# First queries and keys of the second layer loaded beside the scan's end, and a new order for that layer

## The chip, the core and the metric

The kernel runs on one core of a Trainium2 chip. The core has five engines with instruction streams of their own: TensorE (PE; its weight loads are listed as PEld), VectorE (DVE), ScalarE (ACT), GpSimd (POOL) and SyncE (SP), which here issues nearly all DMAs. Each engine runs its stream in order and waits on semaphores; the DMAs of a queue are moved by 16 DMA engines. The metric is the time of one execution in microseconds on the device, lower being better.

## What is computed

Two layers stand one behind the other, each added to its input. x has 4 batches of 1024 tokens with 512 features.

The first layer is a selective scan over time with 16 states and 1024 inner channels:

```python
def step(h, inputs):
    ad, bd, xt, ct = inputs
    h = jnp.clip(h * ad[:, :, None] + bd[:, :, None] * xt[:, None, :], -10.0, 10.0)
    yt = jnp.einsum('bd,bdh->bh', ct, h)
    return (h, yt)
...
x = x + (ys + D * xn) * silu(gate) @ W_out.T
```

In outline, the second layer is attention with 16 heads of 32 features, with weights that are scaled per batch by a style:

```python
q = heads(einsum('bsh,oh->bso', x, q_weight) * q_dc[:, None, :])
k = heads(einsum('bsh,oh->bso', x, k_weight) * k_dc[:, None, :])
v_flat = einsum('bsh,oh->bso', x, v_weight) * v_dc[:, None, :] * s2[:, None, :]
attn = softmax(einsum('bhqd,bhkd->bhqk', q, k) * scale)
out = einsum('bhqk,bhkd->bhqd', attn, heads(v_flat))
return out @ w (scaled by w_dc) + v_flat @ u (scaled by u_dc)
```

In the second layer x is first scaled by the style and normalized over its features.

## The kernel before

**The scan.** `mamba` goes through the 1024 time steps in chunks of 64. For each step SP spreads a row of 256 KB over the partitions (`rep<-xnd`, function `spread`, six buffers), ScalarE scales it (`u`), VectorE makes the step (`g`), and TensorE sums four steps into `yb`. Behind the scan come, for each half chunk, transposes (`yt`), a product with the gate on VectorE or GpSimd (`xnT`), and the output projection (`po`), whose sum with x goes to DRAM (`x1d`).

**The head of the second layer.** Beside the last chunks runs `overlapped` (L1050), which prepares what of the second layer is possible already: the norm of the first blocks of batch 0 (`hio`, `hntr`, result `xs`), the scale factors (`hraw`, `dc`), and queries and keys of two groups of four heads for the first 512 tokens. Each such result is split into two parts, a high one (`hfh`) and the rest (`hfl`), and written to a bounce buffer in DRAM (`bnc`). Its instructions take place among those of the scan by the scheduler's choice. Buffers of 128 x 4096 numbers named w00, w01, w10 and w11 are shared by both layers: in the scan they hold the input weights, afterwards `xs` (w00, w01), the values (w10) and the output weights `wo` (w11).

**The second layer.** `attention` works in units: 4 batches of 8 units, each one group of four heads by 512 queries. For each unit there are

- loads of queries `qs` (three buffers), keys `ks` and key differences `ds` (two buffers each, for the two units of a group) from the bounce buffer; a load takes three DMAs, one for each third of 96 partitions (`stack`, L1350). A 97th row holds the negative row maximum for the queries (`qs<-mt`) and ones for the keys (`ks<-oned`);
- the row maxima: `dps` and `mps` on TensorE, `r` on ScalarE and VectorE (`peaks`), for the very first unit a plain maximum `mx` (`first_peaks`, L1297);
- scores `st`, exponents `p`, sums `s` on GpSimd (VectorE takes one head of four), products with the values `avs`, the ratio `ao`.

Between these lies other work, which the text calls fillers: norm (`io`, `st`, `mv`, `ntr`), queries and keys (`heads`: `wqr`, `wqh`, `wql`, `qps`, `fh`, `fl`), values (`raw`, `bc`, `wh`, `wl`, `vps`), the skip product (`skip`: `vt`, `ups`, with weights `wo`) and the output product.

**What sets the order.** The order of the second layer is written by a planner, `Loom` (L44): generators name an engine, a duration and conditions, and the planner picks the one that can start first, ties by rank. The instructions of each engine are then chained in that order (`Lane`), so that on the chip each engine runs the planned sequence whatever the real durations are. The ranks of the fillers come from `DUE` and `DUE0` (batch 0), counted in exponents, 32 to a unit; `EXTRA` is a latency that the planner adds for work off the main chain.

At the start of the layer the planner isn't asked. The rows of ones and the loads of the first queries and keys are issued by SP ahead of everything else, at a high priority:

```python
with tc.high_priority(offset=FIRST):
    for t in ks:
        nc.sync.dma_start(out=f32(t[96:97].rearrange("o h t -> o (h t)")), in_=E.oned)
    ...
    for nm, dst in (("q", qs[0]), ("k", ks[0][:, :, 0:512])):
        for y in stack(0, 0, nm, 0, dst):
            pass
```

The buffers `qs` and `ks` belong to pools of the second layer, which lie where pools of the scan were.

Of the kernel before, what the change touches and what calls it, by code (L numbers as in the profile page):

```python
# [39 lines left out]
def f32(ap):  # L40
    return ap.bitcast(F32)
# [811 lines left out]
EARLY = -10  # L853
CORE = ("scores", "exponent", "groups", "alone", "sums", "ratio", "peaks", "peak", "row", "first_peaks", "first_peak")
LAT1 = {'PE': 0.3, 'ACT': 0.4, 'DVE': 0.8, 'POOL': 0.8, 'SP': 4.0, 'L1': 0.0}
EXTRA = {'PE': 0.1, 'ACT': 0.3, 'DVE': 0.3, 'POOL': 0.5, 'SP': 1.0}
MARGIN = 0.9
END = (12, 3, 12)
LAND = {"q": 5.5, "k": 9.0, "d": 10.5}
DUE = {'norm': (-206, 14.4), 'heads': (-96, 24), 'v0': (-108, 2.2), 'v1': (12, 2.2), 'skip': (100, 8), 'out': (266, 9)}  # L860
DUE0 = {'heads': (-72, 24), 'v0': (-10, 2.2), 'v1': (40, 2.2)}
FIRST = 1000000

class Env:
# [23 lines left out]

    def values(self):
        self.v = self.sp.tile([128, 8, DM], F32, tag="w10", name="v")
        self.wv = self.sp.tile([128, 2, 2, 4, 256], F32R, tag="w11", name="wv")

    def out_weights(self):
        self.wo = self.sp.tile([128, 2, 2, 4, 256], F32R, tag="w11", name="wo")
# [153 lines left out]
def overlapped(E, *L0):  # L1050

    wk, pm, E.pe, E.vec, E.act = L0
    E.light = True
    raws, turns = [0], [1]

    def tile(name, shape, dt=F32):
        n = int(np.prod(shape[1:]))
        if name in ("g", "qps") and (name == "g" or turns[0] % 3 == 0):
            turns[0] += name == "qps"
            t = pm[0].tile([128, 512], F32, tag=pm[2], name="hg")  # L1060
        elif name == "ntr" or name == "qps" and turns[0] % 3:
            turns[0] += 1
            t = pm[0].tile([128, 512], F32, tag=pm[1], name="h" + name)
        else:
            if name == "raw":
                raws[0] ^= 1
            tag, full, dd, bufs = {
                "raw": ("xh", [128, 4, 256], F32R, 2) if raws[0] else ("xl", [128, 4, 256], F32R, 2),
                "small": ("cv", [128, 4, 64], F32, 3), "bc": ("cv", [128, 4, 64], F32, 3),
                "s1": ("xc", [128, 2, 2, 4, 32], F32, 4), "io": ("xr", [128, 2, 4, 67], F32, 5),  # L1070
                "st1": ("st", [128, 4, 6], F32, 2), "mv1": ("mv", [128, 4], F32, 2),
                "wqr": ("xr", [128, 2, 4, 67], F32, 5), "tmp": ("xc", [128, 2, 2, 4, 32], F32, 4),
                "wqh": ("xc", [128, 2, 2, 4, 32], F32R, 4), "wql": ("xc", [128, 2, 2, 4, 32], F32R, 4),
                "fh": ("tok", [128, 1024], F32R, 2), "fl": ("tok", [128, 1024], F32R, 2)}[name]
            t = wk.tile(full, dd, tag=tag, name="h" + name, bufs=bufs)
            d = " ".join("abcd"[:len(full) - 1])
            t = t if dd == dt else f32(t)
            t = t.rearrange("p %s -> p (%s)" % (d, d)) if len(full) > 2 else t
        t = t[:shape[0], 0:n]
        return t.rearrange("p (a b) -> p a b", a=shape[1]) if len(shape) == 3 else t  # L1080

    E.tile = tile
    E.inputs()
    yield from norm_x(E, 0, range(4))
    yield from demodulation(E)
    yield from heads(E, 0, (0,), (0, 1))
    yield from norm_x(E, 0, range(4, 7))


def attention(ctx, E, T, out, begun):  # L1090
# [34 lines left out]
    def mark(*key):  # L1125
        done[key] = loom.end

    def have(*key):
        return lambda: done.get(key)
# [12 lines left out]
    def parts():  # L1142

        j = frs.take()
        return j, tuple(work(x, [128, 512], 1, F32R, f"{x}{j}") for x in ("fh", "fl"))

    def place(u, qq=0, kp=0, h=0):
        return 32 * u + 16 * qq + 4 * kp + h

# [2 lines left out]
    def scores():  # L1152
        for u in range(NU):
            for qq, kp, h in np.ndindex(2, 4, 4):
                yield "PE", 0.25, sts, have("row", u), have("k", u // 2, 0), have("k", u // 2, 1)
                i = sts.take()
                q, k = qs[u % 3], ks[u // 2 % 2]
                st = pst.tile([128, 2, 256], F32, tag="t", name="st")
                for e in range(2):
                    kb = 2 * kp + e  # L1160
                    pe.matmul(st[:, e, :], k[0:97, h, kb * 128:kb * 128 + 128], q[0:97, h, qq * 256:qq * 256 + 256], start=True, stop=True)
                loom.add(exponent(u, qq, kp, h, i, st), place(u, qq, kp, h))
            mark("scores", u)

# [119 lines left out]
    def row(u, m1):  # L1284
        yield "PE", 0.15, bank_of
        i, tr = bank([16, 128], "mtr")
        pe.transpose(tr, m1.rearrange("p h q -> p (h q)"), ident)
        yield "ACT", 0.2, mts
        j, mt = mts.take(), work("mt", [16, 128], 1, F32R)
        acte.activation(mt, tr, AF.Identity, scale=-1.0)  # L1290
        bank_of.give(i)
        yield "SP", 0.6
        sp.dma_start(out=f32(qs[u % 3][96:97].rearrange("o h (q c) -> o (h q) c", c=128)), in_=f32(mt))
        mts.give(j)
        mark("row", u)

    def first_peaks():  # L1297

        q, k = qs[0], ks[0]
        mx = work("mx", [128, 4, 4, 2], 1)  # L1300
        for o, h, qb in np.ndindex(2, 4, 4):
            yield "PE", 0.24, bank_of, have("q", 0), have("k", 0, o)
            i, ps = bank([128, 512], "mps")
            pe.matmul(ps, q[0:96, h, qb * 128:qb * 128 + 128], k[0:96, h, o * 512:o * 512 + 512], start=True, stop=True)
# [12 lines left out]
    def peaks():  # L1317

        for u in range(1, NU):
            m1 = work("m1", [128, 4, 4], 2)  # L1320
            left[u] = 16
            for h, qb in np.ndindex(4, 4):
                n = (u - 1) * 16 + h * 4 + qb
                yield "PE", 0.24, bank_of, past("relu", n - RF), have("q", u), have("k", u // 2, 0), have("d", u // 2)
                i, ps = bank([128, 512], "dps")
                qh = qs[u % 3][0:96, h, qb * 128:qb * 128 + 128]
                pe.matmul(ps, qh, ds[u // 2 % 2][:, h, :], start=True, stop=True)
                loom.add(peak(u, n, i, ps, qh, h, m1[:, h, qb:qb + 1], m1), 2 * n + EARLY)

    def peak(u, n, i, ps, qh, h, m, m1):  # L1330
# [4 lines left out]
        mark("relu", n)  # L1335
        yield "PE", 0.24, bank_of
        i, ps = bank([128, 512], "mps")
        pe.matmul(ps, qh, ks[u // 2 % 2][0:96, h, 0:512], start=True, stop=True)
# [21 lines left out]
    def loads():  # L1360
        for u in range(NU):
# [205 lines left out]
            mark(key, b)  # L1567

    def skip_weight(b):
        yield "SP", 0.01, have("values", b, 1), past("out", b - 1)  # L1570
        for hf in range(2):
            yield from weight("u", b, hf)
        mark("wu", b)
# [5 lines left out]
        mark("wo", b)  # L1579

    def skip(b, tb):
        w = [(E.wo[:, hf, 0], E.wo[:, hf, 1]) for hf in range(2)]
# [12 lines left out]
        i, ps = yield from project(vh, vl, w)  # L1595
        ts.give(k)
        yield "DVE", 0.62
        dve.tensor_tensor(out=x1, in0=ps, in1=x1, op=ALU.add)
# [28 lines left out]
        return rs, ao, j, jo  # L1627

    def output(b, tb, n):
        w = [(E.wo[:, hf, 0], E.wo[:, hf, 1]) for hf in range(2)]  # L1630
# [10 lines left out]
        i, ps = yield from project(ah, al, w)  # L1641
        ts.give(k)
        yield "DVE", 0.62
        dve.tensor_tensor(out=rs, in0=ps, in1=rs, op=ALU.add)
# [6 lines left out]

    def ending(b, tb):

        w = [E.wo[:, :, e] for e in range(2)]

        def products(ps, ah, al, kb):
            for n, (a, e) in enumerate(((ah, 0), (ah, 1), (al, 0))):
                pe.matmul(ps.rearrange("p (h c) -> p h c", h=2), a, w[e][:, :, kb, :], start=kb == 0 and n == 0, stop=kb == 3 and n == 2)
# [37 lines left out]


    loom.end = 0.0
    with tc.high_priority(offset=FIRST):
        for t in ks:  # L1700
            nc.sync.dma_start(out=f32(t[96:97].rearrange("o h t -> o (h t)")), in_=E.oned)
# [12 lines left out]
    loom.add(first_peaks(), -100)  # L1714
    loom.add(style(0), -91)
    for tb in range(begun, NT):
# [69 lines left out]
```

## Time and profile before

| | us |
|---|---|
| median of 3 executions | 2790.56 |
| lowest and highest | 2787.77 and 2792.78 |
| the profiled execution | 2796.49 |
| its span, first to last instruction | 2794.7 |
| PE busy | 2566.8 (92%) |
| ACT busy | 2021.2 (72%) |
| DVE busy | 1994.9 (71%) |
| POOL busy | 2083.1 (75%) |
| last step of the scan ends | 1275.2 |
| first scores of the second layer | 1365.2 |

The profile is of one execution. Busy time is the time in which an engine runs at least one instruction; issuing a DMA isn't counted. "Granted clock" is the share of full speed that TensorE's clock had, here 0.951 in the mean. The chain of waits follows the work that ended last back from the end: at each piece to what released it. In the timeline a group is given with its start, its length, its engine and its tiles (out<-in), and in brackets the idle time of the engine before it with what ended it. Nearly all instructions have the line of a helper, L167, so tiles are what tells them apart.

### The profile page before, as it was taken

What the parts mean: (1) busy time and instruction counts of PE and PEld (TensorE: products, weight loads), DVE (VectorE), ACT (ScalarE), POOL (GpSimd) and SP (SyncE); (2) the same over time, 40 slices, a digit from 0 to 9 for tenths busy, and PEclk for the clock granted to TensorE, in tenths of its full rate; (3) what the DMA queues carried; (4) which work ended last, traced back from release to release, by engine and by line L of the source; (5) the groups of instructions that cost most, each with busy time, mean ns of one, the idle gap of its engine ahead of it and who ended that gap; (6) DMA issues with size and microseconds to landing.
All of it is one profiled execution on the core that took longest, in us unless ns stands there. A gap on an engine that the chain in (4) does not pass through costs nothing.

```text
span 2794.7 us, 54619 instructions
## 1 busy us (share of the span) xinstructions
PE 2566.8 (92%) x18421; PEld 1775.8 (64%) x18421; DVE 1994.9 (71%) x3518; ACT 2021.2 (72%) x3766; POOL 2083.1 (75%) x2365
## 2 busy tenths in 40 slices
PE   7798999999999998886989899989999899999998
PEld 7565565665566665433756677756777667777765
DVE  4778888888878887674557766677567786667665
ACT  5888888888888888663567677667766676676674
POOL 5887788787778787443378888787787787777786
PEclk9899999999999999787989999999999999999998
DMA  5789989999989999895652455344553545345422
GB/s 173 226 239 273 271 267 274 274 265 272 270 250 272 273 276 266 254 252 147 174 130 82 121 141 171 104 127 116 147 144 118 135 124 140 120 121 151 107 58 91
DMA packets 333772, 518.26 MB, mean 185 GB/s; under 512 B 33514, under 2 KB 108586, under 8 KB 333362
## 3 DMA queue, kind: packets, MB, share of 16 engines
q1 hardware_dynamic: 333076, 514.71, 65.1%
q8 instruction: 145, 2.38, 0.4%
q14 instruction: 135, 1.11, 0.1%
q10 hardware_dynamic: 416, 0.07, 0.0%
HBM read 422.35 MB, written 92.05 MB: 184 GB/s over the span
## 4 chain that ended last, share of the span: by engine, by line
PE 43%; DMA 15%; POOL 15%; ACT 11%; DVE 8%; issue 7%; SPq 0%; ACTq 0%; POOLq 0%; DVEq 0%
DMA rep<-xnd 9%; PE avs L167 8%; PE st L167 7%; POOL s L167 5%; ACT u L167 5%; PE ups L167 5%; PE qps L167 4%; DVE g L167 4%; PE mps L167 3%; PE ps L167 3%; POOL tmp L167 3%; PE vps L167 3%; PE dps L167 3%; POOL tm L167 2%; PE po L167 2%
## 5 line engine op out<-in xcount | busy, mean ns | idle before, releaser
L167 DVE CUSTOM_DVE_ANT_0 g<-g,u,hi 128x512 f32<-128x512 f32 x1024 | 820.5, 801 | 209.4 <-ACT u L167 171.3
L167 ACT ACTIVATE p<-st 128x512 f32<-128x512 f32 x1024 | 599.2, 606 | 312.3 <-PE st L167 288.6
L167 ACT ACTIVATE u<-rep,bd 128x512 f32<-128x512 f32 x1024 | 699.4, 689 | 121.5 <-DMA rep<-xnd 67.8
L167 POOL TENSOR_TENSOR s<-s,p 128x512 f32<-128x512 f32 x384 | 538.9, 1420 | 58.1 <-ACT p L167 57.2
L167 DVE CUSTOM_DVE_ANT_0 r<-mps,r 128x512 f32<-128x512 f32 x496 | 334.7, 683 | 271.9 <-PE mps L167 249.7
L167 PE MATMUL ps<-xh,w_in 128*128 128x256 f32 x2048 | 493.4, 317 | 15.2 <-ACT w_in L167 10.5
L167 PE MATMUL st<-qs,ks 97*128 97x256 f32 x2048 | 450.5, 305 | 33.1 <-ACT p L167 24.0
L167 PEld LDWEIGHTS st<-qs,ks 97*128 97x128 f32 x2048 | 350.1, 195 | 152.4 <-ACT p L167 82.8
L167 POOL TENSOR_TENSOR s<-p 128x512 f32<-128x512 f32 x192 | 255.1, 1342 | 202.2 <-PE avs L167 106.9
L167 PEld LDWEIGHTS ps<-xh,w_in 128*128 128x128 f32 x2048 | 344.8, 191 | 91.7 <-issue 65.3
L167 PE MATMUL yb<-g,sy 128*32 128x512 f32 x2048 | 287.9, 633 | 57.7 <-DVE g L167 42.5
L167 ACT ACTIVATE r<-dps 128x512 f32<-128x512 f32 x496 | 298.5, 606 | 42.2 <-DVE m L167 20.5
L167 POOL TENSOR_TENSOR tmp<-tmp,tm 128x256 f32<-128x256 f32 x372 | 272.6, 733 | 73.6 <-ACT tmp L167 44.6
L167 PE MATMUL ps<-xl,w_in 128*128 128x256 f32 x1024 | 290.2, 283 | 0.0
L167 PE MATMUL avs<-p,v 128*32 128x256 f32 x4096 | 269.8, 408 | 2.4 <-ACT p L167 2.3
L167 PE MATMUL mps<-ks,qs 96*128 96x512 f32 x528 | 222.3, 435 | 16.1 <-DMA ks<-bnc 9.7
L167 PEld LDWEIGHTS ps<-xl,w_in 128*128 128x128 f32 x1024 | 196.4, 192 | 30.1 <-issue 30.1
L167 PE MATMUL dps<-ds,qs 96*128 96x512 f32 x496 | 204.4, 413 | 11.6 <-DMA bnc<-fh 5.7
L167 PEld LDWEIGHTS avs<-p,v 128*32 128x32 f32 x4096 | 126.8, 116 | 112.6 <-issue 25.4
L167 POOL TENSOR_SCALAR tm<-xr,c_w_conv 128x256 f32<-128x256 f32 x372 | 182.3, 490 | 20.1
L167 PE MATMUL qps<-xs,wqh 128*128 128x512 f32 x480 | 190.1, 401 | 0.1
L167 PE MATMUL ups<-wo,th 128*128 128x256 f32 x960 | 187.8, 288 | 0.0
(389 smaller groups left out, 4826.2 us busy)
## 6 DMA issues: line engine op xcount, KB each, us to landing
rep<-xnd SPq DMA_DIRECT2D x1024, 256.0 KB, 4.8
qs<-bnc SPq DMA_DIRECT2D x96, 256.0 KB, 4.5
ks<-bnc SPq DMA_DIRECT2D x96, 256.0 KB, 7.6
bnc<-fh SPq DMA_DIRECT2D x76, 256.0 KB, 3.3
bnc<-fl SPq DMA_DIRECT2D x76, 256.0 KB, 3.0
xnd<-z SPq DMA_DIRECT2D x64, 256.0 KB, 4.6
io<-x1d SPq DMA_DIRECT2D x57, 256.0 KB, 3.4
ds<-bnc SPq DMA_DIRECT2D x48, 256.0 KB, 9.0
```

The lines of the kernel that those rows point to most:

```text
L167: i = f(*a, **k)
```

## The change

The change has four parts.

1. A new function `first` takes a buffer in the place w11 while the scan still runs. It writes the row of ones of the keys, and after the queries and keys of the first group are in the bounce buffer, loads both into it, three DMAs each. `overlapped` calls it between the first and the second group. The loads at the start of `attention` go, with their high priority.
2. `scores`, `peaks`, `row` and `first_peaks` read the first unit's queries (`E.q0`) and the first group's first 512 keys (`E.k0`) from there. The keys' rows of ones are written when the keys of a group are first loaded.
3. The output weights `wo` take w11 only when the first group's scores are done: `skip_weight` waits for the scores of unit 1.
4. Due places and a latency of the planner have new values. (The second number of an entry of `DUE0` isn't read: the step comes from `DUE`.)

```diff
-EXTRA = {'PE': 0.1, 'ACT': 0.3, 'DVE': 0.3, 'POOL': 0.5, 'SP': 1.0}
+EXTRA = {'PE': 0.1, 'ACT': 0.3, 'DVE': 0.3, 'POOL': 0.25, 'SP': 1.0}
...
-DUE = {'norm': (-206, 14.4), 'heads': (-96, 24), 'v0': (-108, 2.2), 'v1': (12, 2.2), 'skip': (100, 8), 'out': (266, 9)}
-DUE0 = {'heads': (-72, 24), 'v0': (-10, 2.2), 'v1': (40, 2.2)}
-FIRST = 1000000
+DUE = {'norm': (-206, 14.4), 'heads': (-136, 24), 'v0': (-68, 2.2), 'v1': (12, 2.2), 'skip': (100, 8), 'out': (266, 9)}
+DUE0 = {'heads': (-84, 19.2), 'v0': (30, 2.2), 'v1': (40, 2.2)}
...
-        self.wv = self.sp.tile([128, 2, 2, 4, 256], F32R, tag="w11", name="wv")
+    def first(self):
+        t = self.sp.tile([128, 2, 4, 512], F32R, tag="w11", name="first")
+        self.q0, self.k0 = t[0:97, 0], t[0:97, 1]
+        self.nc.sync.dma_start(out=f32(t[96:97, 1].rearrange("o h t -> o (h t)")), in_=self.oned[:, 0:2048])
+        for nm, dst, order in (("q", self.q0, (0, 0, 1)), ("k", self.k0, (0, 1, 0))):
+            for p, e in enumerate(order):
+                self.nc.sync.dma_start(out=f32(dst[32 * p:32 * p + 32]), in_=self.parts[0, 0, nm, 0][e].rearrange("(h p) c -> p h c", h=4))
+                yield
...
-    yield from heads(E, 0, (0,), (0, 1))
+    yield from heads(E, 0, (0,), (0,))
+    yield from E.first()
+    yield from heads(E, 0, (0,), (1,))
...
+    def queries(u):
+        return qs[u % 3] if u else E.q0
+    def first_half(g):
+        return ks[g % 2][:, :, 0:512] if g else E.k0
...
+                if g < 2:
+                    yield "SP", 0.6
+                    sp.dma_start(out=f32(ks[g][96:97].rearrange("o h t -> o (h t)")), in_=E.oned)
...
-        yield "SP", 0.01, have("values", b, 1), past("out", b - 1)
+        yield "SP", 0.01, have("values", b, 1), past("out", b - 1), have("scores", 1)
+        if b == 0:
+            E.out_weights()
...
-    with tc.high_priority(offset=FIRST):
-        for t in ks:
-            nc.sync.dma_start(out=f32(t[96:97].rearrange("o h t -> o (h t)")), in_=E.oned)
-        for hg in range(2):
-            keys[hg] = E.parts[0, hg, "k", 0]
-            for nm in "qk":
-                mark("part", 0, hg, nm, 0)
-        for nm, dst in (("q", qs[0]), ("k", ks[0][:, :, 0:512])):
-            for y in stack(0, 0, nm, 0, dst):
-                pass
-    done["q", 0] = done["k", 0, 0] = 4.0
+    for hg in range(2):
+        keys[hg] = E.parts[0, hg, "k", 0]
+        for nm in "qk":
+            mark("part", 0, hg, nm, 0)
+    E.parts.pop((0, 0, "q", 0)), E.parts.pop((0, 0, "k", 0))
+    done["q", 0] = done["k", 0, 0] = 0.0
...
-    E.out_weights()
```

More of the change, by code (lines that the diff above doesn't have):

```diff
@@ L1156, in scores @@
                 i = sts.take()
-                q, k = qs[u % 3], ks[u // 2 % 2]
+                q, k = queries(u), ks[u // 2 % 2]
                 st = pst.tile([128, 2, 256], F32, tag="t", name="st")
@@ L1160, in scores @@
                     kb = 2 * kp + e
-                    pe.matmul(st[:, e, :], k[0:97, h, kb * 128:kb * 128 + 128], q[0:97, h, qq * 256:qq * 256 + 256], start=True, stop=True)
+                    pe.matmul(st[:, e, :], (first_half(u // 2) if kb < 4 else k[:, :, 512:])[0:97, h, kb % 4 * 128:kb % 4 * 128 + 128], q[0:97, h, qq * 256:qq * 256 + 256], start=True, stop=True)
                 loom.add(exponent(u, qq, kp, h, i, st), place(u, qq, kp, h))
@@ L1292, in row @@
         yield "SP", 0.6
-        sp.dma_start(out=f32(qs[u % 3][96:97].rearrange("o h (q c) -> o (h q) c", c=128)), in_=f32(mt))
+        sp.dma_start(out=f32(queries(u)[96:97].rearrange("o h (q c) -> o (h q) c", c=128)), in_=f32(mt))
         mts.give(j)
@@ L1297, in first_peaks @@
     def first_peaks():
-        q, k = qs[0], ks[0]
+        q = queries(0)
         mx = work("mx", [128, 4, 4, 2], 1)
@@ L1303, in first_peaks @@
             i, ps = bank([128, 512], "mps")
-            pe.matmul(ps, q[0:96, h, qb * 128:qb * 128 + 128], k[0:96, h, o * 512:o * 512 + 512], start=True, stop=True)
+            pe.matmul(ps, q[0:96, h, qb * 128:qb * 128 + 128], first_half(0)[0:96, h] if o == 0 else ks[0][0:96, h, 512:], start=True, stop=True)
             loom.add(first_peak(i, ps, mx[:, h, qb, o:o + 1], o * 16 + h * 4 + qb), -100)
@@ L1325, in peaks @@
                 i, ps = bank([128, 512], "dps")
-                qh = qs[u % 3][0:96, h, qb * 128:qb * 128 + 128]
+                qh = queries(u)[0:96, h, qb * 128:qb * 128 + 128]
                 pe.matmul(ps, qh, ds[u // 2 % 2][:, h, :], start=True, stop=True)
@@ L1337, in peak @@
         i, ps = bank([128, 512], "mps")
-        pe.matmul(ps, qh, ks[u // 2 % 2][0:96, h, 0:512], start=True, stop=True)
+        pe.matmul(ps, qh, first_half(u // 2)[0:96, h], start=True, stop=True)
         yield "DVE", 0.75
@@ L1581, in skip @@
     def skip(b, tb):
-        w = [(E.wo[:, hf, 0], E.wo[:, hf, 1]) for hf in range(2)]
         yield "PE", 0.48, bank_of, ts, ios, have("wu", b)
@@ L1594, in skip @@
         bank_of.give(i)
-        i, ps = yield from project(vh, vl, w)
+        i, ps = yield from project(vh, vl, [(E.wo[:, hf, 0], E.wo[:, hf, 1]) for hf in range(2)])
         ts.give(k)
@@ L1629, in output @@
     def output(b, tb, n):
-        w = [(E.wo[:, hf, 0], E.wo[:, hf, 1]) for hf in range(2)]
         rs, ao, j, jo = yield from places(b, tb, *[have("ao", b, hg, tb // 2) for hg in range(4)])
@@ L1640, in output @@
             aols.give(jo)
-        i, ps = yield from project(ah, al, w)
+        i, ps = yield from project(ah, al, [(E.wo[:, hf, 0], E.wo[:, hf, 1]) for hf in range(2)])
         ts.give(k)
@@ L1652, in ending @@
     def ending(b, tb):
-        w = [E.wo[:, :, e] for e in range(2)]
         def products(ps, ah, al, kb):
             for n, (a, e) in enumerate(((ah, 0), (ah, 1), (al, 0))):
-                pe.matmul(ps.rearrange("p (h c) -> p h c", h=2), a, w[e][:, :, kb, :], start=kb == 0 and n == 0, stop=kb == 3 and n == 2)
+                pe.matmul(ps.rearrange("p (h c) -> p h c", h=2), a, E.wo[:, :, e, kb, :], start=kb == 0 and n == 0, stop=kb == 3 and n == 2)
         rs, ao, j, jo = yield from places(b, tb, *[have("ao", b, hg, tb // 2) for hg in range(3)])
```

## The prediction

> **What bounds the kernel now.** I read the page's engine table first, then busy time by stretch, then the chain of waits, then the timeline of the handover. On the page TensorE is busy 92% of the span and no other engine over 75%, so an idle TensorE is what a gain has to come from. Its idle time lies in two places: at the handover from the scan to the second layer, and in small pieces all through the layer.
>
> The stretches (us, busy time of each engine, granted clock, DMA share, GB/s):
>
> ```profile
> 1250.00:1270.00 20.00, 18.86 (x78) 8.62 (x78) 13.21 (x17) 15.33 (x26) 8.63 (x7) 1.00 1.04 301
> 1270.00:1280.00 10.00, 5.06 (x32) 2.29 (x30) 6.93 (x14) 4.38 (x7) 4.29 (x5) 1.00 0.41 155
> 1280.00:1295.00 15.00, 11.33 (x28) 5.34 (x28) 5.17 (x20) 4.66 (x7) 3.57 (x5) 0.77 0.12 36
> 1295.00:1305.00 10.00, 0.29 (x4) 0.09 (x2) 0.00 (x0) 1.39 (x3) 2.73 (x3) 0.65 0.88 205
> 1305.00:1317.00 12.00, 9.32 (x17) 4.81 (x17) 11.25 (x18) 2.28 (x3) 4.96 (x4) 0.50 0.35 103
> ```
>
> See the fourth row: for 10 us TensorE works 0.29 and VectorE not at all, while DMA runs at 0.88. Just before that, from 1270 to 1295, the DMA engines were nearly free; and before that, in the scan's last 20 us, they were full (1.04).
>
> SP's issues in the timeline of the same place (start, length, engine, what):
>
> ```profile
> 1293.33 2.21 SPq L1701 DMA_DIRECT2D ks<-oned  x2
> 1295.59 1.27 SPq L167 DMA_DIRECT2D qs<-bnc  x3
> 1296.90 1.38 SPq L167 DMA_DIRECT2D ks<-bnc  x3
> ...
> 1299.44 0.63 SPq L167 DMA_DIRECT2D raw<-in_vT  x1
> 1300.12 0.61 SPq L167 DMA_DIRECT2D bc<-dcd  x1
> ```
>
> And the engines' side of it (in brackets the idle time before the group and what ended it):
>
> ```profile
> 1282.32 9.82 PE L167 MATMUL po<-c_wout,xnT__15706 128*128 128x512 f32 x16 [4.27 <-DVE xnT__15706 L167]
> ...
> 1304.95 8.92 PE L167 MATMUL mps<-ks,qs 96*128 96x512 f32 x16 [9.71 <-DMA ks<-bnc]
> 1305.75 9.65 DVE L167 TENSOR_REDUCE mx<-mps 128x1 f32<-128x512 f32 x16 [12.78 <-PE mps L167]
> ...
> 1308.27 1.27 POOL L167 TENSOR_TENSOR raw<-raw,bc 128x512 f32<-128x512 f32 x1 [10.42 <-DMA bc<-dcd]
> ...
> 1315.33 0.68 DVE L167 BATCH_NORM_STATS2 st<-io 128x6 f32<-128x512 f32 x1
> ...
> 1317.19 0.29 PEld L167 LDWEIGHTS vps<-wl,xs 128*128 128x128 f32 x1 [3.17 <-DVE wl L167]
> ```
>
> Eight DMAs are issued by SP ahead of everything else the layer needs; the first products (mps) wait for the last of them. VectorE then reduces 16 products, and only behind these come the norm of the last block (st) and the split of the value weights (wl), which holds TensorE until 1317.19.
>
> The chain of waits through the layer (start, length, what):
>
> ```profile
> 1261.90 6.97 DMA rep<-xnd
> ...
> 1453.08 7.87 DMA qs<-mt
> ```
>
> Both are transfers that the chain waits for: a spread at the scan's end, and in the layer the 8 KB row of maxima, issued behind nine 256 KB loads. The built order leaves these nine there.
>
> **Part 1: six loads leave the gap and go into the scan.** In the built order the six loads of the first queries and keys stand among the last ten spreads (rep). SP meets them in place of idle time, but the DMA engines are full there: six times 256 KB are 1.57 MB, and at the 301 GB/s of the first row that is 5.2 us. Below, the cost is zero if the spreads had slack to spare; above, 5.2 plus a block of SP: the last query load waits for the landing of the bounce hfl (median 5.3 us), and the last spread is issued behind it, at most some 1.8 us late (5.3 less the two spreads and two loads issued in between). ScalarE waits only 3.9 us for spreads between 1250 and 1275, six times, and twice by 0.2 or less, so part of the delay finds slack: I take +3.5, range 0 to 7. [...] The row has a DMA share of 1.04, and I go by the row.
>
> **Part 2: four products before the last output projection.** The built order puts four mps ahead of po, in the 4.27 us in which TensorE waits for VectorE. At about 0.55 us each (8.92 over 16) they take 2.2 us and are hidden, as long as the loads have landed; the last is issued near 1268 and may land 7.6 us later, before 1278. The po then has a gap of about 2.1 us before it. Here po takes 9.82 for 16, 0.61 each, and the clock in its stretch is 0.77. A shorter gap, 2.52 us ahead of the scan's last product at 1275.27, left the clock at 1.00 in the second row; at the later po's pace of 0.43 the 16 take 6.9. So: 0 to -2.9, and I take -2.9 because 2.1 is nearer to the gap that did no harm. [...]
>
> **Part 3: the gap itself.** Without the six loads and one of the two ks<-oned (2.21 for two), SP reaches raw and bc 3.8 us sooner: 1.1 + 1.27 + 1.38. Raw then leaves at 1295.7, bc at 1296.3. With the landing time of this run, 8.15 us from the issue of bc to its use, GpSimd starts at 1304.5 and gains 3.8 at least. With bc's median 4.7 it starts at 1301. VectorE has its 16 reductions from 1293, and is through at 1302.6 (9.65 later) instead of 1315.4. From 1301 GpSimd does raw, wql, raw, io (four times 1.27) to 1306.1, so st starts at 1306.1 for 1315.33: -9.2. ScalarE's wh follows at 1304.8 (1.04 in the timeline), and wl after st at 1306.8, so the vps that waited until 1317.19 starts near 1308: also -9.2. With the slow landing GpSimd ends at 1309.6, st gains 5.8. Range -5.8 to -10.1 (all of wl's 1.2 saved too); I take -9.2 because the crowd of six loads that made the landing slow is gone. What is late next is the landing of raw and bc. The second ks<-oned now stands ahead of the second group's keys, and so of the first row of maxima: 1.1 us of SP, at no cost, because SP sits idle from 1355.45 to the issue of that row at 1358.03; without this cover the first scores, 1365.2, would be 1.1 later.
>
> **Part 4: the order.** New due places and a smaller latency for GpSimd let the planner set the whole layer anew. Count the products between the first scores of one unit and of the next in both built orders, and price each by this chain's rows: scores 0.48 for four, avs 1.86 for 32, qps 0.70 for three, vps and ups 0.71 for six, mps and dps 0.46 for two. A unit's length is the time between the first exponents of one unit and the next in the trace. The work per unit, before and after: unit 2 31.5 and 24.1; unit 5 31.9 and 37.7; unit 17 38.5 and 42.3; unit 20 29.1 and 23.9; unit 21 38.1 and 45.9; unit 26 37.9 and 26.6. The total is the same, the new order less even: above 38 us it has 28 us, the old one 5. Light units don't get shorter than about 40 us (27.5 us of work in unit 29 took 36.2, 29.1 in unit 20 took 40.2, 31.5 in unit 2 took 40.3), heavy ones take 1.16 of their work (44.8 for 38.5). If nothing is smoothed the order costs (28 - 5) x 1.16 = 26. On the other side, the first batch's skip weights now wait for the second unit's scores and move from units 0 and 1 to 1 and 2, which takes two raw at 1.28 from GpSimd in unit 0; and the stall of 7.87 could go. That bounds a gain at 2.6 + 7.9 = 10.5. From -10.5 to +26 I take 0: units overlap through twelve score buffers, light and heavy neighbours (20 and 21, 4 and 5) even out, and lengths between 27.5 and 40 us of work fit one line almost as well as a floor does.
>
> **Sum.** +3.5 - 2.9 - 9.2 + 0 = -8.6. The profiled execution took 2796.49 around a span of 2794.7; the median shown is 2790.56, and I take the difference from that: 2782.
>
> **Rivals.** *The gap is only moved.* The spreads are delayed in full, SP blocks, the po stays slow, raw lands as late as now: +7 - 0 - 5.8 = +1.2, 2791.8. For it: DMA share 1.04 in the very place. Against it: from 1270 on DMA falls to 0.41 and 0.12, so the delayed part ends at once. That the loads don't move at all is excluded by the built order.
>
> *The uneven order decides (slower).* Place: unit pairs such as 20 and 21, with 45.9 us of TensorE work in one. Price 26, less the 8.6 of the handover: +17.4, 2808. It decides from the point where more than 14.2 of the 26 isn't smoothed (8.6 plus 5.6). For it: units 11 and 19, where all the norm transposes fall together, take 53.4 and 53.8. Against: such lumps exist before as well, and 24 to 29 run at 36 to 47.
>
> **Chances and range.** A change under 0.2%, 5.6 us, can't be told from none in this kernel. Forecast 0.50 (2782; alone, 2766 to 2785), the moved gap 0.17, the uneven order 0.33. Faster 0.50, same 0.17, slower 0.33. The range takes in most of the slower case: 2766 to 2808. The best corner, 0 - 2.9 - 10.1 - 10.5 = -23.5, and the worst, +7 - 5.8 + 26 = +27, are left out as both need every term at its end.
>
> **What would show it.** Right: the idle before the first mps falls from 9.71 to below 3; the vps behind wl starts some 8 us nearer to the last step of the scan; po near 7 us; the last u later by 3 to 4. Wrong: the last u later by over 5; raw waiting for bc as long as now; unit 21 over 52 us and unit 20 still 40, or the layer from first scores to end longer than today's 1429 (2794.7 - 1365.2).

## The result and the profile after

The changed kernel takes 2824.78 us (median of 4, 2820.25 to 2836.27), the kernel before on the same chip 2791.67 (2787.77 to 2796.30): a ratio of 1.0120, 95% interval 1.0098 to 1.0142. It is slower by 33 us where 9 us faster was forecast. The profiled execution took 2825.94 around a span of 2824.1, against 2794.7 before.

The same stretches as before, of the changed kernel (us, busy time of TensorE, its weight loads, VectorE, ScalarE, GpSimd, granted clock, DMA share, GB/s):

```profile
1250.00:1270.00 20.00, 16.36 (x65) 6.69 (x64) 9.84 (x13) 10.25 (x17) 2.53 (x2) 0.96 1.06 282
1270.00:1280.00 10.00, 6.90 (x29) 3.10 (x29) 5.42 (x8) 5.97 (x10) 3.52 (x3) 0.83 0.78 219
1280.00:1295.00 15.00, 11.41 (x33) 5.51 (x32) 7.55 (x26) 3.49 (x5) 5.65 (x7) 0.89 0.14 48
1295.00:1305.00 10.00, 6.24 (x20) 2.97 (x20) 9.41 (x16) 3.66 (x7) 5.98 (x5) 0.88 0.57 172
1305.00:1317.00 12.00, 7.91 (x46) 7.41 (x47) 3.98 (x6) 4.08 (x7) 6.13 (x7) 0.67 0.33 100
```

The hole has gone: in the fourth row TensorE works 6.24 us where it worked 0.29, VectorE 9.41 where it worked nothing. The price stands in the first two rows: ScalarE, which works off the spreads, is down from 15.33 to 10.25 in the scan's last 20 us, with the DMA engines as full as before (1.06 for 1.04), and the second row is still busy with transfers (0.78 for 0.41).

The timeline of the same place, changed kernel:

```profile
1281.47 1.17 PE L167 MATMUL mps<-first 96*128 96x512 f32 x4
...
1285.15 8.80 PE L167 MATMUL po<-c_wout,xnT__15706 128*128 128x512 f32 x16 [2.50 <-DVE xnT__15706 L167]
...
1296.81 5.95 PE L167 MATMUL mps<-first 96*128 96x512 f32 x12
...
1307.80 0.69 DVE L167 BATCH_NORM_STATS2 st<-io 128x6 f32<-128x512 f32 x1 [3.21 <-POOL io L167]
...
1309.67 0.29 PEld L167 LDWEIGHTS vps<-wl,xs 128*128 128x128 f32 x1 [1.72 <-DVE wl L167]
```

The products that waited for wl start at 1309.67 where they started at 1317.19, although the scan's last step ended 3.7 us later (1278.88 for 1275.21). The first exponent comes at 1361.04, 4.7 us earlier than before.

So the handover gains and the kernel loses: from the first exponent to the end the layer takes 1463.1 us, before 1428.9, 34 more. The loss isn't spread evenly. Unit 14 alone is 18.2 us longer (63.0 for 44.8). What happens in it (busy time by stretch, then timeline, changed kernel):

```profile
2045.00:2050.00 5.00, 5.00 (x32) 4.00 (x31) 3.90 (x8) 3.92 (x8) 5.00 (x5) 1.00 0.08 28
2050.00:2055.00 5.00, 3.02 (x17) 2.43 (x16) 5.00 (x1) 2.85 (x6) 5.00 (x5) 1.00 0.14 52
2055.00:2060.00 5.00, 0.00 (x0) 0.00 (x0) 5.00 (x1) 0.00 (x0) 5.00 (x6) 0.70 0.77 210
2060.00:2065.00 5.00, 3.69 (x12) 2.87 (x12) 4.55 (x9) 1.20 (x2) 0.10 (x1) 0.50 0.01 3
```

```profile
2049.40 1.28 POOL L167 TENSOR_TENSOR s<-p 128x512 f32<-128x512 f32 x1
...
2049.69 10.96 DVE L167 TENSOR_TENSOR s<-p 128x512 f32<-128x512 f32 x1
2050.65 1.28 POOL L167 TENSOR_TENSOR fh<-fh,fl 128x512 f32<-128x512 f32 x1
2051.90 2.50 POOL L167 TENSOR_TENSOR s<-s,p 128x512 f32<-128x512 f32 x2
...
2058.70 1.40 POOL L167 TENSOR_TENSOR s<-s 128x256 f32<-128x256 f32 x2
2060.57 0.68 DVE L167 CUSTOM_DVE_ANT_0 r<-mps,r 128x512 f32<-128x512 f32 x1
...
2061.31 0.79 PE L167 MATMUL dps<-ds,qs 96*128 96x512 f32 x1 [8.29 <-DVE m L167]
```

One addition on VectorE, of a form whose shortest takes 0.63 us, takes 10.96. It begins while GpSimd is in the middle of a row of instructions without a pause (5.00 of 5.00 us, three stretches running), and it ends 0.55 us after that row does. Everything behind it waits: r on VectorE, dps on TensorE (8.29 us idle), and the granted clock is 0.50 when TensorE comes back. Both operands of this addition lie in SBUF. The reductions r, which read one operand from PSUM, never take over 0.69 us, 496 of them before and 496 after.

Take together VectorE's instructions over 2.5 us in the layer: before 5 of them, 27 us; after 11, 61 us. Of TensorE's idle times over 1 us, those that overlap such an instruction in time sum to 16 us before and 44 after. This was the first theory: **the new order puts GpSimd's work back to back around VectorE's additions**. Its rivals were the uneven units that the prediction had named, and the new handover itself.

### The profile page after: what moved, and what is told of

It is laid out like the page before. It is cut to its first block, busy times and chain, and to the rows that moved or that the text cites. A ratio compares the mean times of both kernels' runs of the same rounds, so it can differ in the third digit from the quotient of the medians.

```text
span 2824.1 us, 54587 instructions
## 1 busy us (share of the span) xinstructions
PE 2576.7 (91%) x18421; PEld 1778.8 (63%) x18421; DVE 2022.7 (72%) x3518; ACT 2019.1 (71%) x3766; POOL 2070.9 (73%) x2365
## 4 chain that ended last, share of the span: by engine, by line
PE 45%; DMA 16%; ACT 12%; POOL 11%; DVE 9%; issue 7%; SPq 1%; ACTq 0%; POOLq 0%; DVEq 0%
DMA rep<-xnd 10%; PE avs L167 8%; PE st L167 8%; PE ups L167 6%; ACT u L167 5%; DVE g L167 5%; PE qps L167 4%; POOL s L167 4%; PE mps L167 3%; PE dps L167 3%; POOL tmp L167 3%; PE ps L167 3%; PE vps L167 3%; ACT p L167 2%; POOL tm L167 2%
## 5 line engine op out<-in xcount | busy, mean ns | idle before, releaser
L167 PE MATMUL st<-qs,ks 97*128 97x256 f32 x1952 | 432.5, 307 | 34.3 <-ACT p L167 27.9
L167 PEld LDWEIGHTS st<-qs,ks 97*128 97x128 f32 x1952 | 334.6, 196 | 154.3 <-ACT p L167 91.2
L167 ACT ACTIVATE r<-dps 128x512 f32<-128x512 f32 x496 | 300.8, 610 | 66.4 <-PE dps L167 38.1
L167 PE MATMUL mps<-ks,qs 96*128 96x512 f32 x480 | 202.7, 427 | 6.2 <-DVE m L167 4.8
```

Of the source, the lines that this page charges most:

```text
L167: i = f(*a, **k)
```

## The experiments

Each ratio is to the kernel before, run between the others on the same chip. "Layer" is the time from the first exponent to the end in the one profiled execution, and "long" the sum of VectorE's instructions over 2.5 us there.

### Which part loses

*structure*: the new handover and the old due places, except one shift without which the planner finds no order.

```diff
-EXTRA = {'PE': 0.1, 'ACT': 0.3, 'DVE': 0.3, 'POOL': 0.25, 'SP': 1.0}
+EXTRA = {'PE': 0.1, 'ACT': 0.3, 'DVE': 0.3, 'POOL': 0.5, 'SP': 1.0}
...
-DUE = {'norm': (-206, 14.4), 'heads': (-136, 24), 'v0': (-68, 2.2), 'v1': (12, 2.2), 'skip': (100, 8), 'out': (266, 9)}
-DUE0 = {'heads': (-84, 19.2), 'v0': (30, 2.2), 'v1': (40, 2.2)}
+DUE = {'norm': (-206, 14.4), 'heads': (-96, 24), 'v0': (-108, 2.2), 'v1': (12, 2.2), 'skip': (100, 8), 'out': (266, 9)}
+DUE0 = {'heads': (-74, 24), 'v0': (-10, 2.2), 'v1': (40, 2.2)}
```

> The changed kernel with the old EXTRA, DUE and DUE0 (but heads of DUE0 at -74 in place of -72): the new handover under an order made by the old places. Theory (GpSimd's back-to-back work holds up VectorE's adds in the new order): the layer is as long as before, 1425 to 1435 us from first exponent to end, the handover gains 4 to 9, so 2782 to 2790; VectorE instructions over 2.5 us sum to at most 40 us. Rival (the structure costs: skip weights that wait for the second unit, loads in the scan): 2810 or more. Rival (uneven order): 2782 to 2790 as well.

1.0067 (1.0042 to 1.0092), layer 1459.5, long 47.4. *order_alone*: the kernel before with the three new lines and nothing else.

> The kernel before with the new EXTRA, DUE and DUE0 and nothing else changed. Theory: the loss is the order's, so 2815 to 2835, and VectorE instructions over 2.5 us sum to 50 us or more, against 27 in the kernel before. Rival (structure): 2785 to 2800. If the order differs from that of the changed kernel and the time is near 2791, the sum of long VectorE instructions should be near 27 again; if the time is high and that sum is low, the theory falls.

1.0154 (1.0111 to 1.0197), 2839.82 us (a little over its bounds), layer 1469.8, long 63.6. *old_latency*: the changed kernel with only EXTRA put back.

> The changed kernel with EXTRA of GpSimd back at 0.5, the new due places kept. Theory: time follows the long VectorE instructions of whatever order comes out; if the smaller latency packs GpSimd's work and is the cause, 2782 to 2795 with a sum under 40; if the due places are, 2815 or more with a sum over 50. Rival (uneven order from the new due places): 2815 or more with a low sum.

1.0184 (1.0147 to 1.0221), layer 1490.8, long 50.5. So the order alone loses what the whole change loses, and putting the old latency back doesn't bring the time back. But structure, whose due places are the old ones but for one, loses as well, and its order isn't the old one: the planner is so sensitive that a shift of two exponents redraws the layer. Hence *before_redrawn*, the kernel before with that shift alone:

```diff
-DUE0 = {'heads': (-72, 24), 'v0': (-10, 2.2), 'v1': (40, 2.2)}
+DUE0 = {'heads': (-74, 24), 'v0': (-10, 2.2), 'v1': (40, 2.2)}
```

> The kernel before with one number changed: heads of DUE0 -74 in place of -72, a shift by two exponents of 1024, which makes the planner set the rest of the layer anew. Theory (any new order loses the luck of the old one, whose long VectorE instructions sum to only 27 us): 2805 to 2830, ratio 1.005 to 1.014, with a sum of 40 us or more. Rival (the new due places are bad in themselves, a neighbouring order of the old places isn't): within 0.3% of before, 2785 to 2800.

1.0136 (1.0103 to 1.0170), layer 1467.1. So a redraw, a new order that comes of a change without a meaning, costs as much as the change does. Yet its long instructions sum to 32.9 us only, under the 40 that the theory asked for: the stalls on VectorE can't be all.

The last doubt on this question is removed by *same_order*. It has the new handover, but planner, places and latencies of before; the second unit reads its keys from their old buffer, loaded behind raw and bc, so that the output weights may take their place after the first unit. ScalarE, VectorE and GpSimd then run the old sequence through the layer, instruction for instruction in the trace.

```diff
+    def first_half(u):
+        return ks[u // 2 % 2][:, :, 0:512] if u else E.k0
...
+        if (b, nm, hf) == (0, "v", 0):
+            for t in ks:
+                sp.dma_start(out=f32(t[96:97].rearrange("o h t -> o (h t)")), in_=E.oned)
+            bnc = E.parts.pop((0, 0, "k", 0))
+            for p, e in enumerate((0, 1, 0)):
+                sp.dma_start(out=f32(ks[0][32 * p:32 * p + 32, :, 0:512]), in_=bnc[e].rearrange("(h p) c -> p h c", h=4))
```

> The new handover under the very order of the kernel before: planner, due places and latencies are those of before, so ScalarE and GpSimd run the same sequence through the whole layer. The first unit reads queries and keys loaded beside the scan's end; the second unit reads the keys from their old buffer, whose three loads (and the rows of ones) SP issues behind raw and bc; the output weights take the place when the first unit is done. Theory (the order loses, not the handover): first exponent 8 to 10 us nearer to the last step of the scan, that step later by 3.5 to 7, the layer 1425 to 1432 long, so 2 to 7 us faster than before, ratio 0.9975 to 0.9995. Rival (the new handover itself unsettles the layer): slower than before, 1.002 or more.

0.9989 (0.9968 to 1.0010), layer 1425.2, and the same five long instructions at the same places as before (27.1 us). The handover costs nothing in the layer; the redrawn order is the loss.

### What a redrawn order loses by

*pool_waits*: the changed kernel in its own order, with GpSimd's next instruction made to wait for VectorE's addition.

```diff
+                if self.eng is self.tc.nc.gpsimd and Lane.port is not None:
+                    self.tc.add_manual_dep(i.ins, Lane.port, AFTER, reason="the port first")
+                    Lane.port = None
...
-            add.tensor_tensor(out=s, in0=P[u, qq, 0, h][1] if first else s, in1=P[u, qq, kp, h][1], op=ALU.add)
+            i = add.tensor_tensor(out=s, in0=P[u, qq, 0, h][1] if first else s, in1=P[u, qq, kp, h][1], op=ALU.add)
+            if h in VADD:
+                Lane.port = i.ins.name
```

> The changed kernel in its own order, but GpSimd's next instruction waits for VectorE's add of three of the four adds of a head's sum (192 waits in all). Theory: no such add takes over 2.5 us any more, their mean falls from 1.26 us to near 1.0; the stall of unit 14 (63 us) goes back to some 45, and the kernel gains 10 to 25 against the changed one, 2800 to 2815, less what GpSimd loses by waiting. Rival (uneven order): adds get shorter but the time doesn't fall, 2820 to 2840.

1.0064 (1.0038 to 1.0090): 15 us gained. VectorE's additions by tile, count, and shortest, median and longest time in ns; the kernel before, the changed kernel, then pool_waits:

```profile
L167 DVE TENSOR_TENSOR s<-s,p x128: 674/938/5103, 1381.9 to 2777.0; 128x512 f32<-128x512 f32 x128
L167 DVE TENSOR_TENSOR s<-p x64: 627/988/1803, 1374.0 to 2766.7; 128x512 f32<-128x512 f32 x64
```

```profile
L167 DVE TENSOR_TENSOR s<-s,p x128: 669/1136/6925, 1375.5 to 2805.8; 128x512 f32<-128x512 f32 x128
L167 DVE TENSOR_TENSOR s<-p x64: 627/978/10958, 1368.7 to 2795.5; 128x512 f32<-128x512 f32 x64
```

```profile
L169 DVE TENSOR_TENSOR s<-s,p x128: 676/1085/1869, 1366.4 to 2783.7; 128x512 f32<-128x512 f32 x128
L169 DVE TENSOR_TENSOR s<-p x64: 628/873/1792, 1359.7 to 2773.3; 128x512 f32<-128x512 f32 x64
...
  POOL s L169: 64.4, 61
```

The longest falls from 10.96 to 1.87 us with the order unchanged, and unit 14 from 63.0 to 48.0. GpSimd's additions wait 64.4 us for it in 61 places (last line: who waited for these instructions, us and times), and still the kernel gains. That VectorE is held up by GpSimd's unbroken work, and that this costs time, is thereby shown. *before_pool_waits*, *after_all_waits* and *structure_all_waits* let GpSimd wait also for the fourth addition and for VectorE's mv, wl, wo and tl, each marked in the same way:

> The kernel before in its own order, with GpSimd's next instruction made to wait for VectorE's instructions of two SBUF operands (adds of sums, mv, wl, wo, tl). A control: the order before has 17 us of TensorE idle time beside long VectorE instructions (after has 44). Theory: a gain of 0 to 15 us, 2775 to 2793, VectorE instructions over 2.5 us nearly gone. Rival (the waits themselves are what gains, or cost): the gain is as large as for the changed kernel, or the kernel loses over 10 us.

0.9977 (0.9961 to 0.9993), layer 1422.0, long 3.1.

> As pool_waits (the changed kernel in its own order), and GpSimd also waits for the fourth add and for VectorE's mv, wl, wo and tl. Theory: the 14.6 us of long VectorE instructions left there go as well, TensorE's idle beside them falls by some 7, and the time falls to 2798 to 2810. Rival: those waits hold GpSimd up as long as they help VectorE, 2811 to 2825.

1.0071 (1.0041 to 1.0102), layer 1441.4, long 9.5: no better than pool_waits in time.

> The run structure (new handover, order of the old places) with the same waits of GpSimd. Theory: of the 32 us of TensorE idle time that stand beside long VectorE instructions there, most go, and with the clock that they cost the kernel gains 15 to 35 on structure: 2780 to 2800, with a handover 8 to 11 us shorter than before that would make it the fastest so far. Rival (the loss of structure has other causes): 2805 or more.

1.0040 (1.0023 to 1.0058), layer 1438.4, long 2.8. It gains 7.5 us, not 15 to 35, and its interval overlaps that of structure. The rival stands: with the stalls gone, structure and the changed kernel still have a layer 16 and 19 us longer than before_pool_waits. So the stalls make up only a part of the difference between the old and the new order. By the times it is the 15 us gained on the new order less the 6 gained on the old, some 8 us of 33, though the intervals taken together allow nothing or twice as much; by the layers of the single profiles it is 15 of 34 (34 less the 19 left).

In what is left another wait stands out. The changed kernel at the third batch's end, SP's queue and then the engines:

```profile
2469.73 1.32 SPq L167 DMA_DIRECT2D qs<-bnc  x3
2471.09 3.00 SPq L167 DMA_DIRECT2D ks<-bnc  x6
2474.16 3.50 SPq L167 DMA_DIRECT2D ds<-bnc  x3
2478.51 0.34 SPq L167 DMA_DIRECT2D io<-resd  x1
2479.67 0.38 SPq L167 DMA_DIRECT2D aol<-aod  x1
```

```profile
2489.36 0.62 ACT L167 CAST th<-aol 128x512 fp32r<-128x512 f32 x1 [8.29 <-DMA aol<-aod]
...
2490.53 0.80 PE L167 MATMUL st<-qs,ks 97*128 97x256 f32 x2 [4.61 <-ACT p L167]
2491.11 1.27 POOL L167 TENSOR_TENSOR s<-s,p 128x512 f32<-128x512 f32 x1 [7.39 <-ACT p L167]
```

The load aol is issued behind twelve loads of 256 KB and lands 9.7 us later; ScalarE stands at the cast th for 8.29 us, and all exponents stand behind it in its queue. The same happens at the ends of the first two batches (7.41 and 6.65 us). *after_aol_late* and *structure_aol_late* tell the planner a later landing (10.0 us as below, and 9.5), with the waits of GpSimd kept:

```diff
-            yield "SP", 0.6, aols
+            yield "SP", 0.6, 10.0, aols
```

> after_all_waits, with the planner told that a load aol lands 10 us after its issue in place of 5, so that ScalarE's cast th comes later in its sequence (a new order follows from the eighth unit on). Theory (half of the loss is VectorE behind GpSimd, much of the rest is ScalarE held at th<-aol: 7.1, 6.2 and 7.6 us in after_all_waits, with 12.5 us of TensorE idle): those three waits fall under 3 us, and the time to 2795 to 2805. Rival (these waits are hidden or come back elsewhere): 2808 to 2825.

1.0064 (1.0044 to 1.0083), layer 1445.3. The three waits are gone, the time isn't: TensorE's idle times over 1 us fall from 55.4 to 36.1, but the short ones and the busy time grow by as much. The theory fell here.

> structure_all_waits, with the same lateness (9.5 us) of aol for the planner. There one such wait stands (6.8 us of ScalarE, 6.5 us of TensorE idle in the tenth unit). Theory: it goes, 2793 to 2801, less or more by what the redrawn order brings. Rival: 2804 or more.

0.9999 (0.9983 to 1.0015), layer 1427.2: here it held. As each of the two is also a new draw, the pair settles nothing on these waits.

So back to the rival of the prediction. Take the planner's own durations of TensorE's work between the first scores of one unit and of the next (scores, mps and dps priced at 0.235 us each), and sum over units 1 to 30 what exceeds 38 us; the old order has 89 us. Among the kernels with the waits:

```
                     over 38 us   ratio
before_pool_waits        89       0.9977
structure_aol_late      100       0.9999
structure_all_waits     107       1.0040
after_aol_late          116       1.0064
after_all_waits         117       1.0071
```

This is a correlation found afterwards. It leaves something over: without the waits structure and before_redrawn have the same sum, 107, and take 1.0067 and 1.0136, with intervals that don't touch, although before_redrawn has less in long instructions (32.9 for 47.4). Neither measure explains that pair.

Two orders were then chosen by the plan alone and forecast, even_waits and uneven_waits, both same_order_waits (below) with other due places and the changed kernel's smaller latency for GpSimd:

```diff
+DUE = {'norm': (-194, 14.4), 'heads': (-86, 28), 'v0': (-50, 2.2), 'v1': (12, 4), 'skip': (92, 10.7), 'out': (250, 15)}
+DUE0 = {'heads': (-74, 24), 'v0': (-10, 2.2), 'v1': (44, 2.2)}
...
+DUE = {'norm': (-216, 18), 'heads': (-96, 26), 'v0': (-68, 6), 'v1': (20, 3), 'skip': (100, 12), 'out': (280, 11)}
+DUE0 = {'heads': (-84, 24), 'v0': (-10, 2.2), 'v1': (40, 2.2)}
```

"Port" in the first of the two is, as in the code's `Lane.port`, the author's name for VectorE's waiting beside GpSimd's work; that a port is behind it, no run here shows.

> same_order_waits with other due places, so a fresh order, chosen out of some 300 by the plan alone: TensorE's planned work above 38 us per unit sums to 84 us over units 1 to 30 (before 89, structure 107, the changed kernel 117). Theory (port and unevenness are all that a new order loses by): a layer of 1418 to 1430 us, time 2780 to 2792, ratio 0.995 to 0.999. Rival (the old order is good for a cause of its own, a fresh one loses 15 to 30 even with the waits): 2800 to 2818.

> As even_waits, but an order whose planned TensorE work above 38 us per unit sums to 122 us (spread of the units 8.8 us, against 5.3 before and 7.1 in the changed kernel). Theory: from the four kernels with waits (0.75 us of layer for each us above the old order's 89) a layer longer by 24 us, 2805 to 2830. Rival (evenness has no part): the same as even_waits within 8 us.

even_waits (84 us): 1.0023 (1.0003 to 1.0043), layer 1431.0. uneven_waits (122 us): 1.0224 (1.0187 to 1.0261), layer 1481.7. The even one is a redraw that loses only 5 us, where five without the waits lost 18 to 55; but against the old order with the same waits (0.9977) it loses 13, and at 2795.45 it isn't within its bounds of 2780 to 2792. The uneven one loses far more than forecast (2850.86); its unit 8, with 61 us of planned work, took 66.3 where same_order_waits took 46.8, and the end after unit 31's first exponent is 18 us longer. The two came out in the forecast direction, then, but that unevenness is the cause isn't shown, and it has no fixed price for each us: 0.75 was too little, uneven_waits with 122 has a layer 40 us longer than after_all_waits with 117, and 84 against 89 says nothing.

### What the handover is worth

*same_order_waits* adds the waits to same_order:

> The same, and GpSimd's next instruction waits for VectorE's instructions of two SBUF operands, as in before_pool_waits. Theory: the gains add, 6.5 us from the waits and 2 to 7 from the handover: 2778 to 2785, ratio 0.995 to 0.9975, the fastest here. Rival: the waits' gain is gone or the handover costs, 0.998 or more.

0.9977 (0.9963 to 0.9991), no better than the waits without the new handover. Its reason is at the scan's end, and the times of one pair of profiles hide it, for the scan's earlier part varies from run to run (step 1000 ends between 1236 and 1257 us). From step 1000 to the last step the four kernels without the six loads take 26.6 to 27.8 us (mean 27.0), twelve kernels with them 34.3 to 38.1 (mean 36.0). In the chain of waits of the changed kernel transfers follow one another there (start, length, what):

```profile
1247.53 5.53 DMA xres<-in_x
...
1253.08 7.05 DMA first<-bnc
...
1260.15 7.99 DMA hio<-x1d
...
1268.19 8.23 DMA rep<-xnd
```

Each is issued when the one before has landed, 0.02 to 0.05 us behind it: one of the six loads has become a link in it. *late_loads* is same_order_waits with the six behind the last spread:

```diff
+            LAST[:] = [i.ins.name]
...
+                self.tc.add_manual_dep(i.ins, LAST[0], BEHIND, reason="behind the last spread")
...
-    yield from E.first()
...
+    with tc.high_priority(offset=1000000):
+        for _ in E.first():
+            pass
```

> same_order_waits, with the six loads of the first queries and keys (and their row of ones) issued right behind the last spread of the scan in place of among the last ten. Theory (their place costs the scan 9 us): from step 1000 to the last step 27 us again in place of 36; the first products land some us later, but the layer's start depends on raw and bc, so the first exponent stays within 81 to 86 us of the last step: 4 to 9 us faster than same_order_waits, 2779 to 2784, ratio 0.994 to 0.9965. Rival (the scan's end is late for another cause, or the later loads take the gain back): 2786 to 2792.

From step 1000 to the last it takes 27.4 us again; the first exponent stands 85.6 us behind the last step. SP's queue in late_loads:

```profile
1260.21 4.61 SPq L172 DMA_DIRECT2D rep<-xnd  x5
1264.87 4.10 SPq L911 DMA_DIRECT2D first<-bnc  x6
```

0.9973 (0.9956 to 0.9990), 2784.36 us: the fastest of all by its ratio, though 0.9965 had been the most that was expected, and same_order_waits lies within the interval. That the place of the loads is what delays the scan is shown; whether it is SP's waiting or the DMA engines' load wasn't tried apart. The traces say that much: the last spread leaves SP 23.6 us after step 1000 in the changed kernel, before 18.9, so 4.7 us of the 6.5 between these two profiles are there when the last spread is issued.

late_only and after_late make the same edit in same_order and in the changed kernel.

> same_order (new handover, old order, no waits of GpSimd) with the six loads behind the last spread. Theory: the first exponent stands 85 to 86 us behind the scan's last step (before 90.5 to 91.6), the scan ends as before (27 us from step 1000), the layer is 1425 to 1430: some 5 us faster than before, ratio 0.997 to 0.999. Rival (the handover is worth nothing): 0.9995 or more.

late_only: 0.9985 (0.9970 to 0.9999), 26.5 us from step 1000, first exponent 87.4 us behind the last step, later than the 85 to 86 expected.

> The changed kernel in its own order, with the six loads behind the last spread. Theory: from step 1000 to the last step 27 us in place of 34 to 38, the first exponent 85 to 86 behind it in place of 82: 3 to 6 us off, ratio 1.0095 to 1.011 against 1.0118. Rival (no gain): 1.0118 or more.

after_late: 1.0109 (1.0090 to 1.0128). The scan's end takes 27.5 us, but the first exponent stands 87.8 us behind it, not 85 to 86; the gain is within the interval.

## Why the prediction was wrong

**Part 4, the order, taken at 0, is the step that failed.** It is +34 in the profile, beyond the upper bound of 26 (its own factors give 26.7). For a loss the text had weighed the planned work per unit and nothing else, and let it even out to nothing, as if the old order were one of many equals. The runs show that it isn't: five other orders without the waits (order_alone, old_latency, structure, before_redrawn and the changed kernel's own) give layers of 1459 to 1491, the old order 1425 to 1429. The old order is a good draw, and what redrew it lost 18 to 55 us. That VectorE's work would stall behind GpSimd wasn't a term of the sum at all, though the trace of before had five such instructions of 5 to 7 us. It is some 8 us of the difference by the times, 15 by the layers. What is left, 19 to 25 us, is the order's as well, for same_order doesn't lose it. The unevenness that the rival named may be part of it; how much, and what the rest is, stays open.

**Part 1, +3.5 (0 to 7), was mis-sized: +9.0**, twelve kernels against four. The pair of profiles shows 3.7 and seems to confirm it; that is chance, the changed kernel's run being 2.9 us ahead at step 1000. The upper bound counted the bytes and one wait of SP, which was to hold the last spread for 1.8 us at most; in the pair it is issued 4.7 us later. Other loads of SP stand in the same queue and land later too: xres and hio take 5.53 and 7.99 us in the chain above, 3.77 and 6.74 before.

**Part 2, -2.9, was too much.** Four mps do stand in the gap, and 2.50 us are left behind them, near the 2.1 counted; but po takes 8.80 for 9.82: -1.0. The prediction took a short gap for harmless because one of 2.52 had left the clock at 1.00 in the stretch before. The gap of 2.50 here, from 1282.64 to 1285.15, didn't (changed kernel, columns as above):

```profile
1280.00:1282.00 2.00, 1.53 (x11) 1.28 (x11) 0.59 (x2) 0.59 (x1) 1.53 (x3) 1.00 0.69 249
1282.00:1284.00 2.00, 0.64 (x3) 0.19 (x1) 2.00 (x8) 0.00 (x0) 2.00 (x2) 1.00 0.35 114
1284.00:1286.00 2.00, 0.85 (x2) 0.62 (x3) 2.00 (x4) 0.00 (x0) 0.45 (x1) 0.90 0.00 0
1286.00:1288.00 2.00, 2.00 (x3) 0.69 (x3) 1.45 (x8) 0.66 (x1) 1.11 (x2) 0.50 0.00 0
1288.00:1290.00 2.00, 2.00 (x5) 0.79 (x4) 0.49 (x3) 1.38 (x3) 0.55 (x1) 0.74 0.00 0
```

The granted clock is 1.00 when the gap begins and 0.50 in po's first part: po's weight loads take 0.34 us until 1288.24 and 0.19 from 1289.07 on, 3.9 us at the slow pace. So the length of a gap didn't settle it; what sets the two gaps apart, no run here shows. That the filled gap saves 2.9 was wrong: po took 1.0 less.

**Part 3, -9.2, was right.** The vps behind wl stand 30.8 us behind the scan's last step, before 42.0: 11.2 nearer, where parts 2 and 3 together said 12.1. At the first exponent 9.8 of it is left (twelve kernels 78.7 to 82.9 us behind the last step, mean 81.0, against 90.5 to 91.6 in four, mean 90.8).

Sum of the handover: +9.0 - 9.8 = -0.8, not -8.6. So for this part the rival "the gap is only moved" (+1.2) was right, for the reason that it gave, the spreads' delay; that po stays slow was right too, that raw lands late was not.

**The rival "the uneven order decides" had the sign and the part of the kernel, not the place or the price.** Units 20 and 21 take 34.4 and 53.2 us after, 40.2 and 46.2 before: together 87.6 for 86.4, so this pair evens out as the prediction had said. The time was lost elsewhere, most in unit 14.

Of the signs named: the idle before the first mps fell below 3, and vps came nearer, as said; po near 7 didn't come; the last u is 4.1 later (1276.51 for 1272.41), near the 3 to 4 named, by the same chance as in part 1. Counted from step 1000 it is 7.0 later, past the 5 that was named as a sign of being wrong. Of the signs for wrong, the layer longer than 1429 was the one that told, and unit 21 over 52 came without unit 20 at 40.

## What to carry to other kernels

Where a planner or scheduler sets the order, a change to any of its inputs buys a new draw: measure first what a meaningless redraw costs (here 1.0136), keep the order fixed to judge the rest, and compare intervals inside a run (step 1000 to the last step) rather than one absolute time. A VectorE addition with both operands in SBUF took 10.96 us here beside a whole row of GpSimd's instructions: where the plan assumes a pause, make GpSimd wait, which cost nothing here (0.9977 on the old order, 15 us gained on the new). The six loads cost the scan 9.0 us among its last spreads, where the DMA share was 1.06 and their 1.57 MB at the 301 GB/s of before come to 5.2 us; behind the last spread they delayed nothing in it (27.4 us from step 1000, for a mean of 27.0 without them).

## What the hardware showed

VectorE's addition waited through a whole row of GpSimd instructions, 10.96 us over the one that was running and nine more. All six additions s of over 2.5 us in the changed kernel end 0.55 us after the end of a GpSimd instruction, as if each took its usual time only then. They are the exception: of the 192 additions of 128x512, 182 see no GpSimd instruction start beside them or one, 10 see two to nine (before 187 and 5). What decides between the two cases, no run here shows.

The addition of 10.96 us has both operands in SBUF, and nine GpSimd instructions that started after it were through before it. The reductions r, with one operand in PSUM, stay at 0.69 us at most. No run here changes only where an operand lies, so that the place decides isn't shown.

After 8.29 us without work TensorE came back at a granted clock of 0.50 in the following 5 us, and a product qps took 0.63 us there where it took 0.40 before the stall, so this stall cost more than its length.
